# Layers 2 and 3 of a four-layer graph kernel take their chunks in the order 2, 3, 1, 0, so that layer 2 begins with the chunk that layer 1 ended on

## The chip, the cores and the metric

The kernel runs on one core of one Trainium2 chip. The metric is the device time of one execution in microseconds (us). A profiled execution has in addition a span, from its first to its last instruction, and a record of every instruction and DMA in it. Engines: PE multiplies matrices (PEld loads its weights), DVE is the vector engine, ACT the scalar engine, POOL is GpSimd, and SP issues most DMAs.

## The reference

Four layers work on the same 3327 nodes with 64 features. Each reads the same dense, weighted adjacency matrix `adj` (3327 x 3327, float32, 44 MB) in full, and each ends in a residual layer normalisation:

```python
x = layernorm(x + L0(x, adj, W))                 # mean over neighbours: (adj @ x) / (rowsum + 1)
x = layernorm(x + L1(x, adj, weight, bias))      # hyperbolic: sum over j of w[i,j] * logmap(x_i, x_j), expmap
x = layernorm(x + L2(x, adj, W, b))              # (adj @ x + x) / deg, concat, relu, unit norm
x = layernorm(x + L3(x, adj, weight, bias))      # the last 100 neighbours of each row, weights 0.5 ** rank

# L3
mask = (adj != 0); rank = cumsum(mask, axis=1)   # w = mask * 0.5 ** (k - pos) for the last 100 set places
out  = w @ (x @ weight) + bias
```

## The kernel before

**Tiles.** The matrix is transposed, padded to 3328 x 3328 and cut into four chunks of 832 columns (the nodes i whose sums are formed) by 26 blocks of 128 rows (the nodes j that are summed over). A *pair* is two row blocks of one chunk, [128, 2, 832] float32, 832 KB; one DMA on SP (`load_adj`, L278) fetches it into one of four `adj` buffers. A layer needs 4 x 13 pairs, and layers 0, 1 and 2 fetch all 52 each. `aggregate_pair` (L434) adds a pair to a chunk's sums in PSUM: four float32 products, eight records at L439, 1.40 us of PE.

**Layer 0** takes the chunks in `ORDER` (0, 3, 1, 2) and also makes the ranks of layer 3 for chunks 0, 1 and 2 (uint8, `rank`).

**Layer 1** (`layer1_far`, L785; the arm `layer1_near` isn't run on this input) goes over `ORDER` again, the pairs of each chunk in the order of `PAIRS` (0 to 5, 10, 11, 12, 6, 7, 8, 9). For each block PE makes v (L793) from `wt` and `ut`, DVE makes p (L804) from v and the pair, ACT and POOL or DVE make s (L817 to L819, L812), and PE adds s up (L824). p has 4 buffers, s has 9. At a chunk's end `keep1` (L832) copies the sums out, `own1` (L842, products at L847) makes a product with the nodes' own features from `ut`, and `epilogue1` (L853, products at L861) makes the new features of that chunk's nodes in `xr`. `GROUPS` says which blocks of nodes have both chunks they need: 0 to 5 with chunk 0, 20 to 25 with 3, 6 to 12 with 1, 13 to 19 with 2.

**Layer 2** needs all of `xr` to end a sum, but it can begin: nine of the 13 pairs of its first chunk (`EARLY`) don't touch the blocks of layer 1's last group, 13 to 19. `load_ahead2` (L1135) fetches the first six when layer 1 issues its last step, four into the `adj` buffers and two into `wt`; `begin2` (L1143) adds two of them (`BEGUN`) ahead of the last `epilogue1` and seven behind it. Then `layers_2_and_3` (L1153) goes over the chunks in `ORDER`, which starts with chunk 0. For each chunk it loads and adds pairs, `prologue2` (L1158) prepares the nodes' own part at the 11th pair, `keep_sums` copies the sums, and `epilogue2` (L1180, products at L1187) makes the input of layer 3, `x3`, and splits it into three bfloat16 `parts` (L1221 to L1224).

**Ranks of chunk 3** are made in layer 2, in its second chunk, over the pairs from 12 down to 0: `mask` (L459, DVE) marks the set places, `count` (L496, PE, L505) counts along the rows, `carry` (L491, DVE) hands a pair's count to the next, ACT writes the ranks (L515) into `uw`, which is `ut` and `wt`. `last_rows` (L521) mends the last row of each block by small DMAs on POOL (L530, L531, L537) and three DVE instructions (L533 to L535).

**Layer 3** consists of 52 *pieces* (`piece`, L1245): one pair of blocks of one chunk, twelve bfloat16 products (L1263) of `parts` with `bits`, which ACT or DVE expand from the ranks (L1242, L1243; ten buffers, tag `m16`, shared with the masks). A piece needs the `parts` of its two blocks for all columns. Twelve pieces lie between the pairs of layer 2's third chunk, eight in its fourth, and 32 behind it.

**Order.** The program is written as one sequence, with `issue_after` for wishes. At build a scheduler lays out the instructions of each engine, and buffer pools and PSUM banks (`Banks`) decide which must wait for which; each engine then works through its own list in order, and a waiting instruction holds what stands behind it. Memory of a pool that is closed is taken by the next pool, whose first users then wait for the last users of the old one.

Of the kernel before, what the change touches and what calls it, by code (L numbers as in the profile page):

```python
# [40 lines left out]
GROUPS = {0: (0, 6), 3: (20, 26), 1: (6, 13), 2: (13, 20)}  # L41
GB = 7
# [5 lines left out]
BEGUN = 2  # L48
# [56 lines left out]
LAST_PAIR = 9  # L105
# [3 lines left out]
def four_gnn_layers_kernel(  # L109
# [164 lines left out]
    def load_adj(c, jp, t=None):  # L274

        if t is None:
            t = adjp.tile([P, 2, CH], FP, name="adj", tag="adj")
# [35 lines left out]
    def blocks_of(c):  # L313
        return (*GROUPS[c], GROUPS[c][1] - GROUPS[c][0])

# [118 lines left out]
    def aggregate_pair(acc, x, a2, jp, first, last, behind=None):  # L434


        for k in (1, 0):
            for h in range(2):
                issued = nc.tensor.matmul(  # L439
                    acc[h * D : (h + 1) * D, 0:HC], lhsT=x[:, 2 * jp + k, 0:D],  # L440
                    rhs=a2[:, k, bass.ts(h, HC)],
# [6 lines left out]
    class Ranks:  # L448
# [8 lines left out]
        def mask(self, jp, a2):  # L457
            mask = self.mp.tile([P, 2, CH], U16, name="mask", tag="m16").bitcast(BF)
            issued = nc.vector.tensor_scalar(mask, a2, 0.0, None, op0=ALU.not_equal)  # L459
# [325 lines left out]
    def layer1_far(banks, begin2):  # L785

        with tc.tile_pool(name="l1w", bufs=1) as wp:

            def far_v(c, jb, after):
# [11 lines left out]
            def far_factors(v, a, engine):  # L801

                p = wp.tile([P, CH], FP, name="p", tag="p", bufs=4)
# [3 lines left out]
                s = wp.tile([P, CH], FP, name="s", tag="s", bufs=L1_AHEAD + 3)  # L807
# [85 lines left out]
            waiting, last, side, total, summed = [], None, None, NCH * NB, None  # L893
            for start in range(0, total + L1_AHEAD, L1_GROUP):
                group = range(start, start + L1_GROUP)
                made = []
                for i in group:
                    if i < total:
                        if i % 2 == 0:
                            c, jp, a2 = next(pairs)  # L900
                        jb = 2 * jp + i % 2
# [4 lines left out]
                for i in group:  # L906
# [12 lines left out]
                    if i == total - 1:  # L919
                        loaded2 = load_ahead2()  # L920
# [21 lines left out]
                for i in group:  # L942
# [6 lines left out]
                    if n == NCH - 1 and j >= NB - OWN1_LAST:  # L949
                        assert side is None  # L950
                        k = 3 * (j - NB + OWN1_LAST)
                        if k == 0:
                            own = banks.one(0)
# [3 lines left out]
            issued = summed  # L957
            issued = begin2(banks, 0, loaded2, issued)
            for done in epilogue1(ORDER[-1], own, 1, issued):
                pass  # L960
            begin2(banks, 1, loaded2, issued)
            return done
# [172 lines left out]
    def load_ahead2():  # L1135


        views = [None] * 4 + [
            wt[:, bass.ts(k, 2 * CH)].rearrange("p (b i) -> p b i", b=2) for k in range(2)
        ]  # L1140
        return [load_adj(ORDER[0], PAIRS[k], view) for k, view in enumerate(views)]

    def begin2(banks, part, loaded, behind, kept={}):  # L1143

        if part == 0:
            kept["acc"] = banks.pair(0)[:, 0, :]
        for i in range(0, BEGUN) if part == 0 else range(BEGUN, EARLY):
            jp = PAIRS[i]
            a2 = loaded.pop(0) if loaded else load_adj(ORDER[0], jp)
            issued = aggregate_pair(kept["acc"], xr, a2, jp, i == 0, False, behind)  # L1150
        return issued

    def layers_2_and_3(banks, acc, done):  # L1153

        with tc.tile_pool(name="late", bufs=1) as late, tc.tile_pool(name="l2m", bufs=10) as mp:
# [273 lines left out]
```

## Time and profile before

| what | value |
|---|---|
| median of 3 runs | 537.79 us (536.46 to 537.92) |
| profiled execution: time, span | 536.65 us, 534.9 us |
| read from HBM | 134.27 MB |
| loads of a pair | 156, of 832 KB |
| layer 1's last sum ends (L824), last epilogue's `xr` (L783) ends | 345.9 us, 365.9 us |
| layer 2's first chunk summed, first count of ranks starts | 374.5 us, 383.9 us |
| second chunk's products (L1187) start | 421.9 us |
| last pair added | about 482 us |

Times in the table's lower half are from the span's start. Groups of instructions are named by line, engine and operation, then output<-input. A row of the chain or timeline begins with the start and the duration in us. A busy PE is not a PE at its peak, since products overlap; the spacing of its records tells more. Where a wait has several causes, the profile names the last.

### The profile page before, as it was taken

The page shows a single profiled execution, that of the slowest core. Times are in us where ns is not written, and L with a number is a line of the kernel's source. Part 1 is how long each engine was busy: PE and PEld are TensorE (multiplying, and loading weights), DVE is VectorE, ACT ScalarE, POOL GpSimd, SP SyncE. Part 2 cuts the span into 40 slices and gives each one's busy share as a digit, 9 for nine tenths or more (in the row PEclk, how much of TensorE's full clock was granted, in tenths as well). Part 3 has the DMA queues.
Part 4 walks back from the last instruction along what each step waited for, and adds up shares of the span by engine and source line. Part 5 has one row for each costly group of instructions (what it writes and reads, how often), then busy time and mean ns, then how long its engine had stood idle before and what let it go on. Part 6 is the DMA issues. An engine that isn't in the chain of part 4 may idle for free.

```text
span 534.9 us, 8471 instructions
## 1 busy us (share of the span) xinstructions
PE 484.1 (90%) x3256; PEld 242.7 (45%) x3256; DVE 389.5 (73%) x707; ACT 334.1 (62%) x393; POOL 176.2 (33%) x150
## 2 busy tenths in 40 slices
PE   5999999998858999998999999997798999999993
PEld 3555444454423334433443353352344675656672
DVE  3575449899669888799789869945699972736834
ACT  1436536786868989788879977500278653236931
POOL 2001101112008888767767875221022020210000
PEclk9999999999989999999999999999999999999997
DMA  8899999899266777767767876879997789980012
GB/s 271 308 363 347 394 399 387 297 317 305 82 229 219 254 257 260 247 208 242 244 201 256 255 227 244 290 227 355 349 320 263 234 288 325 309 319 2 1 28 43
DMA packets 47172, 135.93 MB, mean 254 GB/s; under 512 B 6903, under 2 KB 7007, under 8 KB 47059
## 3 DMA queue, kind: packets, MB, share of 16 engines
q1 hardware_dynamic: 46594, 134.75, 73.6%
q0 software_dynamic: 384, 0.52, 0.4%
q8 instruction: 27, 0.44, 0.4%
q14 instruction: 23, 0.18, 0.1%
q10 hardware_dynamic: 144, 0.03, 0.0%
HBM read 134.27 MB, written 0.85 MB: 253 GB/s over the span
## 4 chain that ended last, share of the span: by engine, by line
PE 49%; DVE 27%; ACT 10%; DMA 6%; issue 3%; POOL 1%; ACTq 0%; POOLq 0%; DVEq 0%
PE one L439 14%; PE two L1263 10%; DVE p L804 7%; PE two L793 6%; DMA adj<-in_adjt_dram 6%; DVE mask L491 5%; PE one L824 5%; PE two L505 5%; DVE s L812 4%; DVE mask L459 3%; ACT s L817 3%; PE two L439 2%; ACT s L818 2%; ACT rank L515 2%; PE two L1187 1%
## 5 line engine op out<-in xcount | busy, mean ns | idle before, releaser
L819 POOL TENSOR_TENSOR s<-s,p 128x832 f32<-128x832 f32 x67 | 130.1, 1956 | 73.3 <-ACT s L818 61.4
L804 DVE SCALAR_TENSOR_TENSOR p<-two,adj 128x832 f32<-128x832 f32 x100 | 101.0, 1018 | 17.8 <-issue 13.3
L793 PE MATMUL two<-uw 64*128 64x416 f32 x416 | 90.1, 545 | 14.3 <-DVE s L812 7.2
L515 ACT ACTIVATE rank<-two,last_bias 128x832 uint8<-128x832 f32 x78 | 71.6, 952 | 45.5 <-DVE mask L491 22.8
L824 PE MATMUL one<-s,xu 128*64 128x416 f32 x416 | 85.2, 524 | 0.0
L439 PE MATMUL one<-adj,x0w 128*64 128x416 f32 x416 | 82.3, 523 | 2.3 <-ACT x0w L644 1.4
L817 ACT ACTIVATE s<-two,far_bias 128x832 f32<-128x832 f32 x67 | 63.7, 950 | 22.7 <-DVE p L804 20.7
L439 PE MATMUL one<-adj,xr 128*64 128x416 f32 x312 | 73.3, 515 | 3.1 <-DMA adj<-in_adjt_dram 3.1
L491 DVE SCALAR_TENSOR_TENSOR mask<-two,minus_last,mask 32x832 bf16<-32x832 f32 x48 | 52.5, 1093 | 24.4 <-PE two L505 20.0
L459 DVE TENSOR_SCALAR mask<-adj 128x1664 bf16<-128x1664 f32 x52 | 55.3, 1066 | 18.8 <-DMA adj<-in_adjt_dram 18.2
L793 PEld LDWEIGHTS two<-uw 64*128 64x128 f32 x416 | 37.5, 189 | 67.0 <-PE one L824 22.6
L1263 PE MATMUL two<-bits,parts 128*64 128x416 bf16 x624 | 67.7, 339 | 0.0
L505 PE MATMUL two<-mask,tri 128*64 128x416 bf16 x416 | 53.5, 346 | 10.9 <-DVE mask L491 8.3
L818 ACT ACTIVATE s<-s 128x832 f32<-128x832 f32 x67 | 60.1, 897 | 1.9
L1263 PEld LDWEIGHTS <-parts 128*64 128x64 bf16 x624 | 41.9, 110 | 20.4 <-issue 5.0
L824 PEld LDWEIGHTS one<-s,xu 128*64 128x64 f32 x416 | 25.8, 136 | 47.5 <-issue 46.6
L505 PEld LDWEIGHTS <-tri 128*64 128x64 bf16 x416 | 24.6, 110 | 45.9 <-issue 24.9
L439 PEld LDWEIGHTS one<-adj,x0w 128*64 128x64 f32 x416 | 29.4, 138 | 34.1 <-issue 23.5
L812 DVE SCALAR_TENSOR_TENSOR s<-two,p 128x832 f32<-128x832 f32 x37 | 37.6, 1016 | 3.0 <-ACT two L809 2.5
L439 PEld LDWEIGHTS one<-adj,xr 128*64 128x64 f32 x312 | 29.4, 137 | 22.4 <-issue 13.6
L1243 ACT ACTIVATE bits<-rank 128x1664 uint16<-128x1664 uint8 x21 | 32.3, 1579 | 9.9 <-PE two L1263 9.8
L809 ACT ACTIVATE two<-two,far_bias 128x832 f32<-128x832 f32 x37 | 34.0, 919 | 5.1 <-DVE p L804 4.9
(235 smaller groups left out, 453.0 us busy)
## 6 DMA issues: line engine op xcount, KB each, us to landing
adj<-in_adjt_dram SPq DMA_DIRECT2D x152, 832.0 KB, 5.6
sums<-in_adjt_dram SPq DMA_DIRECT2D x2, 832.0 KB, 6.0
uw<-in_adjt_dram SPq DMA_DIRECT2D x2, 832.0 KB, 6.5
uw<-in_xt_dram SPq DMA_DIRECT2D x1, 640.0 KB, 10.7
last_a<-in_adjt_dram POOLq DMA_DIRECT2D x4, 84.5 KB, 7.4
out_dram<-o SPq DMA_DIRECT2D x1, 224.0 KB, 3.7
uw<-in_xt_dram SPq DMA_DIRECT2D x1, 192.0 KB, 3.2
out_dram<-o SPq DMA_DIRECT2D x1, 192.0 KB, 2.3
```

The costliest lines, as they stand in the source:

```text
L439: issued = nc.tensor.matmul(acc[h * D : (h + 1) * D, 0:HC], lhsT=x[:, 2 * jp + k, 0:D], rhs=a2[:, k, bass.ts(h, HC)], start=(first and k = ...
L459: issued = nc.vector.tensor_scalar(mask, a2, 0.0, None, op0=ALU.not_equal)
L491: nc.vector.scalar_tensor_tensor(halves(last), ranks.after[P - 32 : P, :, 0:HC], minus_last[P - 32 : P, :], halves(last), op0=ALU.mult, op ...
L505: issued = nc.tensor.matmul(counts[k][rows, h, 0:HC], lhsT=lhsT[:, rows], rhs=mask[:, of, bass.ts(h, HC)], start=lhsT is tri, stop=(k == 1 ...
L515: nc.scalar.activation(halves(ranks.rank[:, 2 * jp + k, :]), counts[k][:, :, 0:HC], AF.Relu, bias=last_bias,)
L793: issued = nc.tensor.matmul(v[:, h, 0:HC], lhsT=wt[rows, bass.ts(jb, P)], rhs=ut[rows, bass.ds(c * CH + h * HC, HC)], start=True, stop=True,)
L804: issued = nc.vector.scalar_tensor_tensor(halves(p), v, 0.25 - 0.5 * FD, halves(a), op0=ALU.add, op1=ALU.mult)
L817: nc.scalar.activation(halves(s), v, AF.Square, bias=far_bias, scale=-2.0)
L818: nc.scalar.activation(s, s, AF.Copy, bias=FG)
L819: nc.gpsimd.tensor_mul(s, s, p)
L824: issued = nc.tensor.matmul(acc[h * D : (h + 1) * D, 0:HC], lhsT=xu[:, jb, 0:D], rhs=s[:, bass.ts(h, HC)], start=first, stop=last,)
L1263: issued = nc.tensor.matmul(acc3[c][h * D : (h + 1) * D, 0:HC], lhsT=parts[:, 2 * jp + b, bass.ts(part, D)], rhs=bits[:, b, bass.ts(h, HC) ...
```

## The change

`ORDER2` = (2, 3, 1, 0) replaces `ORDER` in layers 2 and 3, with groups of blocks to match. Layer 1 still ends with chunk 2; the pairs 6 to 9 of it, its last four, stay in the four `adj` buffers (`kept`) for layer 2's first chunk. Nine pairs are fetched ahead instead of six: three into `ut` and `wt` (the first as soon as its place is free), four as halves into buffers of p and s, two more into `ut`. Two pairs of the second chunk are fetched ahead as halves into buffers of the tag `m16`, whose pool now lies ahead of `late`. One pair instead of two is begun ahead of the last `epilogue1`, whose own product moves to another PSUM bank. The pieces of layer 3 change their order with the groups.

```diff
+ORDER2 = (2, 3, 1, 0)
+GROUPS2 = {2: (13, 19), 3: (19, 26), 1: (7, 13), 0: (0, 7)}
 GB = 7
...
-BEGUN = 2
+BEGUN = 1
...
 L3_BESIDE = 12
-LAST_PAIR = 9
+LAST_PAIR = 3
...
+        if isinstance(t, list):
+            for k in range(2):
+                nc.sync.dma_start(out=t[k], in_=adjt[c, 2 * jp + k])
+            return t
         if t is None:
...
-    def blocks_of(c):
-        return (*GROUPS[c], GROUPS[c][1] - GROUPS[c][0])
+    def blocks_of(c, groups=GROUPS):
+        return (*groups[c], groups[c][1] - groups[c][0])
...
         for k in (1, 0):
+            a = a2[k] if isinstance(a2, list) else a2[:, k, :]
             for h in range(2):
...
                     acc[h * D : (h + 1) * D, 0:HC], lhsT=x[:, 2 * jp + k, 0:D],
-                    rhs=a2[:, k, bass.ts(h, HC)],
+                    rhs=a[:, bass.ts(h, HC)],
                     start=(first and k == 1), stop=(last and k == 0),
...
             mask = self.mp.tile([P, 2, CH], U16, name="mask", tag="m16").bitcast(BF)
-            issued = nc.vector.tensor_scalar(mask, a2, 0.0, None, op0=ALU.not_equal)
+            if isinstance(a2, list):
+                for k, a in enumerate(a2):
+                    issued = nc.vector.tensor_scalar(
+                        mask[:, k, :], a, 0.0, None, op0=ALU.not_equal
+                    )
+            else:
+                issued = nc.vector.tensor_scalar(mask, a2, 0.0, None, op0=ALU.not_equal)
             self.masked.append([self, jp, mask, False])
...
+            def tile_p():
+                return wp.tile([P, CH], FP, name="p", tag="p", bufs=4)
+            def tile_s():
+                return wp.tile([P, CH], FP, name="s", tag="s", bufs=L1_AHEAD + 3)
...
-                p = wp.tile([P, CH], FP, name="p", tag="p", bufs=4)
+                p = tile_p()
                 issued = nc.vector.scalar_tensor_tensor(
...
                 )
-                s = wp.tile([P, CH], FP, name="s", tag="s", bufs=L1_AHEAD + 3)
+                s = tile_s()
                 if engine == "V":
...
             pairs = adj_pairs(first_pairs)
-            waiting, last, side, total, summed = [], None, None, NCH * NB, None
+            waiting, last, side, total, summed, kept = [], None, None, NCH * NB, None, {}
             for start in range(0, total + L1_AHEAD, L1_GROUP):
...
                             c, jp, a2 = next(pairs)
+                            if c == ORDER[-1] and jp in PAIRS[EARLY:]:
+                                kept[jp] = a2
                         jb = 2 * jp + i % 2
...
                     if i == total - 1:
-                        loaded2 = load_ahead2()
+                        loading = load_ahead2(lambda k: tile_p() if k < 4 else tile_s())
+                        loaded2 = next(loading)
                     if late is not None and i >= LATE_AT and not step(late, p_issued):
...
                         if k == 0:
-                            own = banks.one(0)
+                            own = banks.pair()[:, 0, :]
                         own1(ORDER[n], own, (k, k + 1, k + 2), summed)
...
                         keep1(ORDER[n], acc)
-            issued = summed
-            issued = begin2(banks, 0, loaded2, issued)
-            for done in epilogue1(ORDER[-1], own, 1, issued):
+            next(loading)
+            issued = begin2(banks, 0, loaded2, summed)
+            all_of(loading)
+            for done in epilogue1(ORDER[-1], own, banks.turns[1], issued):
                 pass
             begin2(banks, 1, loaded2, issued)
-            return done
+            return done, kept
...
-    def load_ahead2():
-        views = [None] * 4 + [
-            wt[:, bass.ts(k, 2 * CH)].rearrange("p (b i) -> p b i", b=2) for k in range(2)
-        ]
-        return [load_adj(ORDER[0], PAIRS[k], view) for k, view in enumerate(views)]
+    def load_ahead2(more):
...
+        def load(k, t):
+            return load_adj(ORDER2[0], PAIRS[k], t)
+        def view(t, k):
+            return t[:, bass.ts(k, 2 * CH)].rearrange("p (b i) -> p b i", b=2)
+        loaded = [load(k, view(*t)) for k, t in enumerate(((ut, 0), (wt, 0), (wt, 1)))]
+        yield loaded
+        places = [[more(2 * i + k) for k in range(2)] for i in range(4)]
+        loaded += [load(3 + k, t) for k, t in enumerate((*places, view(ut, 1)))]
+        yield
+        loaded.append(load(8, view(ut, 0)))
...
         if part == 0:
-            kept["acc"] = banks.pair(0)[:, 0, :]
+            kept["acc"] = banks.pair(banks.turns[0])[:, 0, :]
         for i in range(0, BEGUN) if part == 0 else range(BEGUN, EARLY):
-            jp = PAIRS[i]
-            a2 = loaded.pop(0) if loaded else load_adj(ORDER[0], jp)
-            issued = aggregate_pair(kept["acc"], xr, a2, jp, i == 0, False, behind)
+            issued = aggregate_pair(kept["acc"], xr, loaded[i], PAIRS[i], i == 0, False, behind)
         return issued
-    def layers_2_and_3(banks, acc, done):
-        with tc.tile_pool(name="late", bufs=1) as late, tc.tile_pool(name="l2m", bufs=10) as mp:
+    def layers_2_and_3(banks, acc, done, there):
+        with tc.tile_pool(name="l2m", bufs=10) as mp, tc.tile_pool(name="late", bufs=1) as late:
             parts = late.tile([P, NB, 3 * D], BF, name="parts")
...
-                b0, b1_, nb = blocks_of(c)
+                b0, b1_, nb = blocks_of(c, GROUPS2)
                 cols = bass.ds(b0 * P, nb * P)
...
                 issued = nc.vector.tensor_reduce(m[:, 0:nb], xs, axis=AX.X, op=ALU.add)
-                if c == ORDER[0]:
+                if c == ORDER2[0]:
                     issue_after(issued, done)
...
-                b0, b1_, nb = blocks_of(c)
-                work, alone = Work(nb), c == ORDER[-1]
+                b0, b1_, nb = blocks_of(c, GROUPS2)
+                work, alone = Work(nb), c == ORDER2[-1]
                 pb = per_block(banks.pair(2), nb, 2 * D)
...
                         for half in range(2):
-                            acc3[ORDER[which + 2 * half]] = two[:, half, :]
+                            acc3[ORDER2[which + 2 * half]] = two[:, half, :]
                     for ahead in range(BITS_AHEAD):
...
-            early = {2: (0, 1, 2), 3: (10, 11)}
-            pieces = [(c, jp) for jps in (*early.values(), (12, 3, 4, 5)) for jp in jps for c in ORDER]
+            early = {2: (7, 8, 9), 3: (10, 11)}
+            pieces = [(c, jp) for jps in (*early.values(), (12, 4, 5, 6)) for jp in jps for c in ORDER2]
             behind = 4 * len(early[2])
             pieces[0:behind] = sorted(pieces[0:behind], key=lambda piece: piece[0] == LATE_RANKS)
-            pieces += [(c, jp) for c in ORDER for jp in (6, 7, 8, LAST_PAIR)]
+            pieces += [(c, jp) for c in ORDER2 for jp in (0, 1, 2, LAST_PAIR)]
             left3 = len(pieces) - 4 * NCH
             beside = range(left3 - L3_LEFT + BITS_AHEAD, left3 - L3_LEFT + BITS_AHEAD + L3_BESIDE)
-            rows = last_rows(late, [(c, rank[:, c]) for c in ORDER if c != LATE_RANKS])
+            ahead = [
+                load_adj(
+                    ORDER2[1], jp, [mp.tile([P, CH], FP, name="a1", tag="m16") for _ in range(2)]
+                )
+                for jp in (NB // 2 - 1, NB // 2 - 2)
+            ]
+            rows = last_rows(late, [(c, rank[:, c]) for c in ORDER2 if c != LATE_RANKS])
             next(rows)
             k = 0
-            for n, c in enumerate(ORDER):
+            for n, c in enumerate(ORDER2):
                 if n > 0:
...
                         continue
-                    a2 = load_adj(c, jp)
+                    if n == 0 and jp in there:
+                        a2 = there.pop(jp)
+                    elif n == 1 and i < 2:
+                        a2 = ahead.pop(0)
+                    else:
+                        a2 = load_adj(c, jp)
                     issued = aggregate_pair(acc, xr, a2, jp, i == 0, i == NB // 2 - 1, counted)
...
                             all_of(rows)
-                    if n in early and i < 4 * len(early[n]):
+                    if n in early and 0 <= i - 3 + n < 4 * len(early[n]):
                         piece(k)
...
                     if n > 0 and i == (1 if n < NCH else 0):
-                        b0, b1_, nb = blocks_of(ORDER[n - 1])
+                        b0, b1_, nb = blocks_of(ORDER2[n - 1], GROUPS2)
                         halves3 = ((b0, b0 + 3), (b0 + 3, b1_)) if n == NCH else ((b0, b1_),)
...
                 if n < NCH:
-                    keep_sums(ORDER[n], acc3[ORDER[n]], 0, True)
+                    keep_sums(ORDER2[n], acc3[ORDER2[n]], 0, True)
...
             kept = {}
-            done = layer1_far(banks, lambda *args: begin2(*args, kept))
-            layers_2_and_3(banks, kept.pop("acc"), done)
+            done, there = layer1_far(banks, lambda *args: begin2(*args, kept))
+            layers_2_and_3(banks, kept.pop("acc"), done, there)
...
```

More of the change, by code (lines that the diff above doesn't have):

```diff
@@ L1381, in four_gnn_layers_kernel @@
             kept = {}
-            loaded = load_ahead2()
-            for part in range(2):
-                begin2(banks, part, loaded, None, kept)
-            layers_2_and_3(banks, kept.pop("acc"), done)
+            with tc.tile_pool(name="l2a_near", bufs=8) as more:
+                loading = load_ahead2(lambda k: more.tile([P, CH], FP, name="ahead", tag="ahead"))
+                loaded = next(loading)
+                next(loading)
+                begin2(banks, 0, loaded, None, kept)
+                all_of(loading)
+                begin2(banks, 1, loaded, None, kept)
+            layers_2_and_3(banks, kept.pop("acc"), done, {})
 def kernel(**inputs):
```

## The prediction

> **What bounds the kernel now.** I read the page first, for which engine is full.
>
> ```profile
> PE 484.1 (90%) x3256; PEld 242.7 (45%) x3256; DVE 389.5 (73%) x707; ACT 334.1 (62%) x393; POOL 176.2 (33%) x150
> PE 49%; DVE 27%; ACT 10%; DMA 6%; issue 3%; POOL 1%; ACTq 0%; POOLq 0%; DVEq 0%
> ```
>
> Over the whole span it is PE, but the 6% of DMA in the chain is a wait, and the change works on loads. So next the span in stages from the end of layer 1 (start:end, length, then busy time of PE, PEld, DVE, ACT, POOL, clock, DMA share, GB/s).
>
> ```profile
> 353.30:365.90 12.60, 10.15 (x56) 3.77 (x56) 9.86 (x36) 1.29 (x3) 3.92 (x7) 1.00 0.98 288
> 365.90:383.90 18.00, 13.53 (x76) 5.51 (x78) 8.97 (x15) 1.29 (x2) 2.19 (x4) 1.00 1.03 365
> 383.90:421.90 38.00, 34.04 (x262) 17.50 (x261) 36.59 (x53) 29.04 (x35) 5.52 (x6) 1.00 0.85 290
> 421.90:485.40 63.50, 63.42 (x493) 41.62 (x495) 34.17 (x64) 23.85 (x26) 10.05 (x10) 1.00 0.82 284
> ```
>
> From 353 to 384 the DMA engines are full and PE is not; from 384 to 422 DVE is full (36.6 of 38 us); from 422 on PE is full, at full clock. A microsecond won before 422 is therefore handed to the end unless a later stage gets a wait of its own. The chain in the first two stages (start, length, what):
>
> ```profile
> by line: DMA adj<-in_adjt_dram 52.4%; PE two L439 33.4%; PE one L439 5.2%; PE two L1187 5.0%; PE two L1165 2.5%; PE two L861 1.1%; PE two L505 0.9%; issue 0.4%
> ...
> 353.30 7.16 PE two L439 x40
> ...
> 360.48 8.05 DMA adj<-in_adjt_dram
> ...
> 368.57 1.62 PE two L439 x8
> ...
> 372.55 8.18 DMA adj<-in_adjt_dram
> ...
> 380.78 1.62 PE one L439 x8
> ```
>
> Loads that could only be issued when PE freed a buffer set the pace until 382, and layer 2's second chunk, which also counts ranks, starts on hungry buffers. Last, the two DVE groups that fill 385 to 421 (busy, mean ns | idle before):
>
> ```profile
> L491 DVE SCALAR_TENSOR_TENSOR mask<-two,minus_last,mask 32x832 bf16<-32x832 f32 x12 | 13.1, 1092 | 0.9 <-PE two L505 0.5
> L459 DVE TENSOR_SCALAR mask<-adj 128x1664 bf16<-128x1664 f32 x9 | 9.5, 1069 | 0.1
> ```
>
> **The change, part by part.** Times "after" are estimates: rows of this trace, moved along the instruction order that the two built programs have. All sums stand against the profiled execution (span 534.9, time 536.65); the median of the runs is 537.79, 1.1 higher, and I subtract from that.
>
> *Own products moved ahead, one pair begun instead of two.* Before: PE finishes layer 1's last L824 at 345.77, starts one pair (L439), waits for xr (L783) until 346.88 because the own product's bank is still held by the previous epilogue, does own1 (L847, 14 records, 1.7 us), finishes two pairs, and only then starts L861 at 351.52. After: own1 has a bank of its own; six of its seven products stand between the last L824s, which delays the last of these by 12 x 0.11 = 1.34 us, to 347.11. ACT's and DVE's copies (L427, L838: 346.86 to 347.95 before) move by as much, to 348.2 and 349.3. One pair (1.40) and the last own product fill PE meanwhile. L861 then starts at 348.8, 2.7 earlier, and its last four wait for 349.3. The DVE chain behind it (L868 at 353.34 to L783's end at 365.94: 12.6 us) is untouched, so xr of the last group is ready at 363.2.
>
> *Nine pairs fetched ahead, four kept.* Four loads of 832 KB go. The nine come into ut, wt and the spent p and s buffers. The first is queued in front of a layer-1 load; the own products and the POOL product it waits for end at 312.8 in this trace, and that layer-1 load is issued at 313.56, so I cost it nothing (if a load slips it has some 10 us: issued 313.56, used near 328). The others follow the last readers of their places: wt's second half at 340.3, the halves in p and s from 340.7 to 346.2 (after L812s), ut at 349.3 and 349.7. Queued loads of this trace land about 2.1 us apart, so they land at 344.7, 346.9, 349.0, 351.1, 353.2, 355.3 and 357.5; PE wants them at 351.8, 353.2 and every 1.4 us on. All are in time: PE's waits for loads, 2.5 us at 361 and 0.4 to 2 before each pair from 366 to 373, go. What is late next is xr: eight pairs end at 350.35 + 8 x 1.40 = 361.6, and PE idles 1.6 us until 363.2. The four kept pairs and the transposes (0.84) end at 369.7; before, the copy of the sums starts at 374.50. This is 4.8 us won.
>
> [...] The row: 832 KB take 4.4 us alone, 2.1 when queued, so loads overlap and the split costs SP's 0.37 us of issue. [...]
>
> *Two pairs of the second chunk ahead.* Their buffers lie where p and s lay; the four half loads wait on SP for the seventh pair (PE, 358.8), with all later loads behind them, and these need kept pairs freed after 364.6 anyway. The halves land at about 362.6 to 366; the next four pairs, issued as kept pairs are freed, at 369 to 375.
>
> *Rows on POOL and DVE.* POOL's memset (L528) ran at 355.2 after L874; now it waits for that same seventh pair, so the six small DMAs behind it start at 359.6 instead of 355.9 and the last is issued at 362.3. They took 7.3 to 7.6 us here beside a full queue, 4.7 for one at 389. So they land between 367.0 and 369.9; L534 and L535 stand on DVE ahead of the third mask and of the sums' copy, which the second-layer products (L1187) need, and these stand on PE ahead of the rest of the chunk. DVE needs about 8.5 us for all that from 363.2 by itself; with the wait the copy ends between 371.7 and 373.4. [...] The row at 389, amid masks on a full DVE, was issued in 0.51 us, as elsewhere: I take nothing.
>
> *Counting starts.* L1187 (1.6), then 3.15 us of pairs: counts start at 376.5 to 378.2 against 383.86. DVE's path to the first carry (L491) has 4.95 us after L1187: 378.3 to 380.0 against 385.15, so 5.2 to 6.9 won, 6.0 in the middle. And two masks and the front of the first epilogue, with an own row product (2.1 + 1.8 + 0.6, less one more "bits", 1.0: 3.5 us), are now done before the full DVE stretch, which was 35.6 us. Bounds for it: 32.0 if DVE stays full, 35.6 if PE, whose own work there is about 32 (13 counts of 1.05, 13 pairs of 1.40), turns the rest into waits. I take 33.6: 2.0 more. Sum 8.0.
>
> *Layer 3's first pieces.* The same 52 pieces (12 products, 1.05 us each) in another order. Half a pair more is done before they begin (-0.7), L1187 has seven blocks (+0.25). New: pair 9 has block 19, which belongs to the second chunk's group, so its pieces need that epilogue's parts (L1224), which were needed only a chunk later. Before, these were done 18.5 us after L1187 (423.4 to 441.9); PE now has 18.5 us of other work in front. Bounds 0 and 3, I take 0.45. Together 0. The tail is the same by count.
>
> **Rivals.** (a) *Hungry loads.* While the kept pairs fill all four buffers, no load of the second chunk but two can fly; its seventh pair's load is issued only at about 377.5. Landing after 4.6 us (the median from 384 to 422) it meets its mask at 382; after 8.0 (the median from 366 to 384) it is 3 us late, and the 2.0 of the stretch go as well: gain 3, 534.8. Against it: nothing else is queued then. (b) *More than I give.* PE has about 16 us of true idle from 346 to 422 (76.1 less 60 of work by the spacing of its records). If the DVE stretch takes 32.0, L1187 waits for nothing and pieces flow, 11 us: 526.8. (c) *Slower: block 19.* DVE has four and ACT two expansions of bits queued ahead of the parts, each waiting for a piece on PE, while PE waits for the parts. From 18.5 us on each microsecond is PE idle on the path; the 8.0 are lost at 26.5, and with 29 the time is 540.3. For it: the chain is new on the path and crosses three engines. Against: the last expansion in front waits for the sixth piece, 12.3 us after L1187, leaving 6 us for some 3 us of work. (d) *The order is not followed*: the built order shows 152 pairs' loads for 156; only waits could undo it.
>
> **How the numbers follow.** The gain of 8.0 gives 537.8 - 8.0 = 529.8. Chances: near the forecast (5.5 to 10.5) 0.55; more, (b), 0.13; less, (a), 0.19; within 0.3%, about what a measurement of this kernel can tell from no change (1.6 us), 0.06; slower, (c) or a layer-1 load slipping, 0.07. The range from 526.0 to 535.5 leaves out about 0.2.
>
> **What would show it.** Right: L783's last end near 363; no wait of L439 for DMA from 345 to 370 but for xr; the first L491 of layer 2 near 379, the last ending near 413; PE full behind it and the end 8 earlier. Wrong: L534 waiting for its rows past 370, masks waiting for loads around 382, or PE waiting for parts before pair 9's pieces.

## The result: about 6 us faster, and the profile after

The changed kernel takes 532.43 us (median of 8 runs, 530.35 to 535.17) beside 538.11 of the kernel before on the same chip: ratio 0.9886, 95% interval 0.985 to 0.9921. Of the 8.0 us forecast, 5.7 came. Its profiled execution has a span of 529.9 us (time 531.74), 5.0 less than before. Three of the kernels below had one execution each in a slower state; it is left out of their times.

The page's lines for the engines and the chain; then the stages (start:end, length, busy time of PE, PEld, DVE, ACT, POOL, clock, DMA share, GB/s), cut at the same work as the stages of before: the last epilogue's first DVE operation, xr ready, the first count of ranks, the second and the third chunk's products.

```profile
PE 482.1 (91%) x3256; PEld 237.7 (45%) x3256; DVE 386.2 (73%) x709; ACT 334.6 (63%) x393; POOL 177.3 (33%) x150
...
PE 46%; DVE 25%; ACT 10%; DMA 8%; issue 6%; POOL 2%; DVEq 0%; POOLq 0%; ACTq 0%
```

```profile
351.30:363.90 12.60, 11.25 (x64) 4.36 (x62) 9.90 (x36) 1.29 (x3) 3.92 (x7) 1.00 0.71 257
363.90:380.60 16.70, 13.81 (x73) 7.09 (x75) 11.35 (x21) 2.38 (x4) 3.14 (x4) 0.90 0.83 277
380.60:417.65 37.05, 34.78 (x269) 18.50 (x266) 32.88 (x48) 29.86 (x35) 5.39 (x6) 1.00 0.85 284
417.65:481.30 63.65, 62.64 (x488) 35.85 (x490) 33.42 (x64) 22.30 (x25) 10.37 (x10) 1.00 0.81 280
```

The page hardly moves; the stages tell. In the first, PE is now busy for 11.25 of 12.6 us (before, 10.15), and what is missing is the wait for xr at its end: the early pairs no longer wait for loads. In the second it is not full (13.81 of 16.7), and its granted clock is 0.90. DVE isn't full in the third (32.88 of 37.05). Two waits are left on PE ahead of the counts (a timeline: start, length, operation, in brackets the idle time before it and what ended it):

```profile
363.92 3.01 PE L448 MATMUL two<-adj,xr 128*64 128x416 f32 x16 [1.37 <-DVE xr L798]
...
374.92 2.90 PE L1220 MATMUL two<-wl,sums 128*128 128x128 f32 x12 [2.87 <-DVE sums L435]
```

The first is the wait for xr that was forecast. The second was not, at this length: L1220 (L1187 before) waits for DVE to copy the sums. Before, DVE had waited for PE at this copy, and the products took 1.60 us:

```profile
374.50 0.58 DVE L427 COPY sums<-two 64x416 f32<-64x416 f32 x1 [4.21 <-PE two L439]
...
382.33 1.60 PE L1187 MATMUL two<-wl,sums 128*128 128x128 f32 x12
```

DVE's timeline after, up to that copy:

```profile
367.40 0.59 DVE L470 TENSOR_SCALAR mask<-a 128x832 bf16<-128x832 f32 x1 [1.99 <-DMA a<-in_adjt_dram]
...
370.24 0.59 DVE L548 TENSOR_SCALAR last_a<-last_a 78x832 f32<-78x832 f32 x1 [1.20 <-DMA last_a<-in_adjt_dram]
...
373.14 1.02 DVE L474 TENSOR_SCALAR mask<-adj 128x1664 bf16<-128x1664 f32 x1
374.19 0.58 DVE L435 COPY sums<-two 64x416 f32<-64x416 f32 x1
```

PE had the sums ready at 370.5. DVE came to the copy at 374.19, because its list has three things in front that need transfers: the third half of a mask (a wait of 1.99 us), the rows (L548 to L550, before L533 to L535; a wait of 1.20), and the mask of the third pair, whose load had landed at 372.22. The chain of waits runs through just this place:

```profile
359.88 0.79 POOL last_more L543
...
362.79 7.33 DMA last_a<-in_adjt_dram
370.24 0.60 DVE last_a L548
...
374.19 0.59 DVE sums L435
374.78 0.14 issue
374.92 2.92 PE two L1220 x12
```

And L1220 then takes 2.90 us for twelve records. The windows ahead of it and over it give the reason: PE is empty in the first (0.13 us busy of 3), and in the second the clock is about halved (0.54).

```profile
372.00:375.00 3.00, 0.13 (x2) 0.11 (x1) 2.94 (x6) 0.19 (x1) 1.49 (x3) 0.89 1.03 403
375.00:378.00 3.00, 3.00 (x14) 2.72 (x16) 0.97 (x2) 0.31 (x1) 0.93 (x1) 0.54 0.81 292
```

Last the two DVE groups of the stretch from the first carry to the last, as shown of before: the waits for loads have not gone (1.8 us of masks), but the twelve carries fit into 34.0 us (382.55 to 416.52) instead of 35.6.

```profile
L506 DVE SCALAR_TENSOR_TENSOR mask<-two,minus_last,mask 32x832 bf16<-32x832 f32 x12 | 13.1, 1093 | 1.5 <-PE two L520 1.2
L474 DVE TENSOR_SCALAR mask<-adj 128x1664 bf16<-128x1664 f32 x8 | 8.2, 1024 | 1.8 <-DMA adj<-in_adjt_dram 1.8
```

### The profile page after: what moved, and what is told of

It reads as the page before. It is cut to its first block, busy times and chain, and to the rows that moved or that the text cites. A ratio compares the mean times of both kernels' runs of the same rounds, so it can differ in the third digit from the quotient of the medians.

```text
span 529.9 us, 8500 instructions
## 1 busy us (share of the span) xinstructions
PE 482.1 (91%) x3256; PEld 237.7 (45%) x3256; DVE 386.2 (73%) x709; ACT 334.6 (63%) x393; POOL 177.3 (33%) x150
## 4 chain that ended last, share of the span: by engine, by line
PE 46%; DVE 25%; ACT 10%; DMA 8%; issue 6%; POOL 2%; DVEq 0%; POOLq 0%; ACTq 0%
PE one L448 12%; PE two L1296 10%; DVE p L825 7%; DMA adj<-in_adjt_dram 6%; PE two L814 6%; PE one L845 6%; DVE mask L506 4%; ACT s L838 3%; PE two L520 3%; DVE s L833 3%; DVE mask L474 3%; ACT s L839 2%; PE two L448 2%; ACT rank L530 2%; PE two L1220 2%
## 5 line engine op out<-in xcount | busy, mean ns | idle before, releaser
L814 PE MATMUL two<-uw 64*128 64x416 f32 x416 | 88.5, 537 | 14.8 <-DVE s L833 7.2
L448 PE MATMUL one<-adj,x0w 128*64 128x416 f32 x416 | 82.7, 524 | 2.6 <-ACT x0w L659 1.4
L448 PE MATMUL one<-adj,xr 128*64 128x416 f32 x296 | 65.6, 514 | 0.9 <-DMA adj<-in_adjt_dram 0.9
L474 DVE TENSOR_SCALAR mask<-adj 128x1664 bf16<-128x1664 f32 x50 | 51.9, 1038 | 18.1 <-DMA adj<-in_adjt_dram 17.4
L1296 PE MATMUL two<-bits,parts 128*64 128x416 bf16 x624 | 64.2, 340 | 0.0
L1296 PEld LDWEIGHTS <-parts 128*64 128x64 bf16 x624 | 37.4, 110 | 23.6 <-issue 6.6
L448 PEld LDWEIGHTS one<-adj,x0w 128*64 128x64 f32 x416 | 29.1, 138 | 35.1 <-issue 23.4
L448 PEld LDWEIGHTS one<-adj,xr 128*64 128x64 f32 x296 | 26.0, 137 | 19.1 <-issue 13.8
```

The costliest lines, as they stand in the source:

```text
L448: issued = nc.tensor.matmul(acc[h * D : (h + 1) * D, 0:HC], lhsT=x[:, 2 * jp + k, 0:D], rhs=a[:, bass.ts(h, HC)], start=(first and k == 1) ...
L814: issued = nc.tensor.matmul(v[:, h, 0:HC], lhsT=wt[rows, bass.ts(jb, P)], rhs=ut[rows, bass.ds(c * CH + h * HC, HC)], start=True, stop=True,)
L1296: issued = nc.tensor.matmul(acc3[c][h * D : (h + 1) * D, 0:HC], lhsT=parts[:, 2 * jp + b, bass.ts(part, D)], rhs=bits[:, b, bass.ts(h, HC) ...
```

## The experiments

**How they are compared.** Layer 1 starts up to 6.5 us earlier or later in one profile than in another, for reasons ahead of the change. So the places in the traces below are counted from the start of layer 1's first sum (165.5 us into the span before, 165.3 after). Time and ratio are of the timed runs, each beside the kernel before on the same chip. The other columns are from one profile of each kernel, and two profiles of one kernel (after and after_again, copy_first and copy_first_2) differ by up to 1.3 us. Line numbers shift by a few between kernels.

| kernel | xr ready | products (L1187, L1220) start | first carry | last carry ends | last instruction | time, us | ratio to before (95%) |
|---|---|---|---|---|---|---|---|
| before | 200.4 | 216.8 | 219.6 | 255.2 | 369.4 | 538.1 | |
| before_with_own | 198.6 | 214.0 | 218.6 | 253.7 | 368.2 | 537.6 | 0.9972 (0.995, 0.9995) |
| after | 198.6 | 209.7 | 217.3 | 251.3 | 364.7 | 532.4 | 0.9886 (0.985, 0.9921) |
| after_again | 198.5 | 209.5 | 217.4 | 250.9 | 363.5 | 533.3 | 0.9891 (0.9855, 0.9927) |
| own_as_before | 204.8 | 215.8 | 221.7 | 256.5 | 368.4 | 534.6 | 0.9901 (0.9858, 0.9943) |
| own_as_before_2 | 200.4 | 210.9 | 216.0 | 252.0 | 363.6 | 532.0 | 0.9857 (0.9813, 0.9902) |
| no_pairs_ahead | 198.6 | 206.8 | 217.7 | 250.9 | 365.5 | 534.1 | 0.9909 (0.9874, 0.9944) |
| not_kept | 198.5 | 209.7 | 216.1 | 249.7 | 364.0 | 532.3 | 0.9891 (0.9852, 0.9931) |
| rows_in_xu | 198.5 | 207.3 | 215.6 | 249.3 | 361.3 | 530.3 | 0.9862 (0.9821, 0.9904) |
| rows_in_xu_copy_first | 198.6 | 206.8 | 216.4 | 250.0 | 363.2 | 530.5 | 0.985 (0.9819, 0.988) |
| rows_early_back_late | 199.9 | 208.1 | 215.0 | 247.5 | 365.1 | 532.8 | 0.9891 (0.9854, 0.9928) |
| copy_first | 198.5 | 206.6 | 213.9 | 247.2 | 359.9 | 529.4 | 0.9821 (0.9785, 0.9856) |
| copy_first_2 | 199.4 | 207.5 | 214.7 | 247.6 | 361.3 | 529.9 | 0.982 (0.977, 0.9871) |
| copy_first_not_kept | 198.6 | 206.6 | 215.8 | 250.0 | 365.0 | 533.7 | 0.9894 (0.9856, 0.9932) |

My theory: what is missing of the forecast is lost between xr and the first carry, by DVE's list ahead of the sums' copy, above all by the rows. Rivals: the second chunk's loads hold the stage in any case; the clock.

**Rows gathered early.** The rows' tiles move into `xu`, which nobody reads after layer 1's last sum.

```diff
-        a = pool.tile(shape, FP, name="last_a")
-        more = pool.tile(shape, U8, name="last_more")
+        if pool is None:
+            flat = xu.rearrange("p b f -> p (b f)")
+            a = flat[0 : shape[0], 0:CH]
+            more = flat[0 : shape[0], CH : CH + CH // 4].bitcast(U8)
+        else:
...
-            rows = last_rows(late, [(c, rank[:, c]) for c in ORDER2 if c != LATE_RANKS])
+            rows = last_rows(None, [(c, rank[:, c]) for c in ORDER2 if c != LATE_RANKS])
```

> The changed kernel, but the last rows of the three ranked chunks are gathered in xu, which nobody needs from 347 on, instead of behind the mask buffers, so their memset and six small DMAs start at about 350 instead of 359.6. Theory rows (they set the start of L1220, 2.9 us late, and take queue time from the second chunk's first loads): the wait of VectorE for last_a goes, the third half of a mask waits under 1 us instead of 2.0, the sums' copy ends near 371.7 instead of 374.8, L1220 starts near 372, takes 1.6 us again instead of 2.9, the first carry comes near 378.5 to 380 instead of 382.55, and the end is 2.5 to 4 us earlier: 528.5 to 530. Rival loads (the third pair's load, landed at 372.2 and masked ahead of the copy, is what holds it): the copy ends at 373.5 or later and under 1.2 us are won. Rival clock (L1220's 2.9 us has nothing to do with the wait in front): it stays at 2.9.

The wait for last_a went, the wait for the third half of a mask fell to 1.01 us, the copy ended 8.7 us after xr instead of 10.9, L1225 waited 0.6 us on PE instead of 2.9 and took 1.58. But the first carry came only 1.6 us earlier, because in front of it DVE now waited 1.91 us for the load of the second chunk's sixth pair, and the time, 530.3, stayed just above the 528.5 to 530 expected. The theory holds for the copy; behind it the rival is next.

**The copy first.** On DVE, the third pair's mask is put behind the sums' copy, the rows' three operations behind that mask:

```diff
                         mask = ranks.mask(jp, a2)
+                        if i == 2:
+                            issue_after(mask, copied)
+                            step(rows, mask)
+                            all_of(rows)
...
-                        if n == 0:
-                            step(rows, made)
-                            all_of(rows)
...
-                keep_sums(c, acc, D, True)
+                copied = keep_sums(c, acc, D, True)
```

> The changed kernel, but on VectorE the sums' copy stands ahead of the third pair's mask and of the rows' three operations, which follow later amid the masks; the rows' DMAs stay where they are. Theory rows (it is the order on VectorE by which late rows reach TensorE): the copy ends near 371.1, L1220 starts without a wait near 372 and takes 1.6 us; the 2.2 us of the rows' operations then fall on the full VectorE, so the first carry comes near 380.5 instead of 382.55, and 1 to 2.5 us are won: 530 to 531.5. If the rows or loads hold the stage by themselves and not through the copy, the first carry stays at 382 to 383 and nothing is won (within 0.7 us).

> The kernel with the copy ahead of mask and rows on VectorE once more, on another chip: again 3 us or more below the changed kernel (ratio to before 0.980 to 0.985), no wait of over 2 us on TensorE but none of its clock falls between 363 and 420, L1223 in 1.6 us.

PE's timeline of copy_first: no wait in front of L1223, and 1.60 us for it.

```profile
367.30 3.01 PE L451 MATMUL two<-adj,xr 128*64 128x416 f32 x16 [1.37 <-DVE xr L801]
...
373.86 1.56 PE L451 MATMUL one<-a,xr 128*64 128x416 f32 x6
375.35 1.60 PE L1223 MATMUL two<-wl,sums 128*128 128x128 f32 x12
```

DVE's timeline of the same kernel, up to the first carry:

```profile
374.08 0.58 DVE L436 COPY sums<-two 64x416 f32<-64x416 f32 x1 [0.48 <-PE two L451]
374.78 1.03 DVE L477 TENSOR_SCALAR mask<-adj 128x1664 bf16<-128x1664 f32 x1
375.72 0.58 DVE L551 TENSOR_SCALAR last_a<-last_a 78x832 f32<-78x832 f32 x1
...
378.36 1.01 DVE L552 SCALAR_TENSOR_TENSOR last_a<-last_more,last_a 78x832 f32<-78x832 uint8 x1
...
382.57 1.09 DVE L509 SCALAR_TENSOR_TENSOR mask<-two,minus_last,mask 32x832 bf16<-32x832 f32 x1
```

Now the copy waits for PE, not PE for the copy. The first carry comes 15.3 us after xr in both runs (18.7 and 18.9 in the changed kernel), 1.3 better than the expected move of 2.0 although the same rows are mended in front of it. At 529.4 and 529.9 us, on two chips, these are the lowest medians of the study: about 3 us below the changed kernel, at the edge of what the intervals separate. From rows_in_xu the intervals don't separate it.

**Both.** Rows in `xu` where the program had them, and the third mask behind the copy.

> Both: the rows gathered early in xu, and the sums' copy ahead of the third pair's mask on VectorE. Theory rows: L1220 starts within 0.3 us of TensorE's being free, near 372, the first carry at 378 to 379, the last carry's end near 412 to 413, which is what the prediction gave, and the time is 528 to 529.5, up to 1 us better than the rows moved alone. Rival loads: with the front gone the masks wait for the loads issued after 377, the stretch from first to last carry grows from 34.0 to 36 or more, and under 2 us are won.

L1228 started 8.2 us after xr with a wait of 0.05 us, as expected; yet the first carry came 17.9 us after xr, and PE's wait was only moved:

```profile
385.25 0.54 PE L523 MATMUL two<-mask,tri 128*64 128x416 bf16 x4 [2.80 <-DVE mask L509]
```

DVE in turn waited 1.97 us for the sixth pair's load. That load took 9.0 us from issue to landing in the changed kernel, 9.2 with the rows early, 10.0 here, but 7.0 in copy_first, where the rows' way back into `rank` (L552) is issued at 380 and later instead of at 374. So the rival is right for this kernel, and there is a guess at why the load is late.

**Rows early, way back late.**

```diff
-        for k, (c, r) in enumerate(chunks):
+        yield None
+        yield [
             nc.gpsimd.dma_start(out=r[P - 1 : P, :, :], in_=more[k * NB : (k + 1) * NB, :])
+            for k, (c, r) in enumerate(chunks)
+        ]
...
+                        if i == 8:
+                            step(rows, mask)
+                            all_of(rows)
```

(`more` lies in `y_last` here, since `xu` is written again before the late transfer.)

> As with the rows gathered early and the copy in front, but the rows' way back into rank (three small DMAs, each into one partition) goes out behind the first epilogue of layer 2, at about 390, instead of at 374. There the load of the second chunk's sixth pair took 9.2 to 10 us from issue to landing with them beside it, and 7.0 in the kernel where they came later. Theory contention: that load lands in 7.5 us or less, VectorE no longer waits 2 us for it ahead of the first carry, which comes 15 to 16 us after xr's end instead of 17.9, and the time is 1.5 to 2.5 us below that kernel's, 528 to 529. Rival (the loads are late by themselves, because they are issued late): the load still takes 9 us or more, first carry at 17.5 or later, time 530 to 531.

The load took 6.9 us and the first carry came 15.05 us after xr: that agrees with the guess of contention. The time does not follow: 532.8. Three things differ from copy_first. xr is ready 1.4 us later; `more`'s memset and three DMAs now stand among POOL's products in layer 1, but copy_first_2, without them, has xr 0.9 later too, so that isn't shown to be their price. DVE, with the last carry at 247.5, is 5.0 us ahead of the next products (252.5; 2.2 in copy_first), for which it then waits: behind the counts PE is the bound. And in the third chunk PE waits twice for loads that took 8.0 and 8.1 us to land, which it does not in copy_first:

```profile
439.11 1.62 PE L451 MATMUL one<-adj,xr 128*64 128x416 f32 x8 [1.66 <-DMA adj<-in_adjt_dram]
441.22 1.26 PE L451 MATMUL one<-adj,xr 128*64 128x416 f32 x5 [0.50 <-DMA adj<-in_adjt_dram]
```

These 2.2 us, with the 2.8 more at the products, are about the 4.9 us by which this profile is longer than copy_first's from the last carry to the end. Why these loads were slow is open.

**Not kept.** The four pairs loaded again, behind the nine.

```diff
...
+            there = {jp: load_adj(ORDER2[0], jp, after=sent[-1]) for jp in there}
             ahead = [
```

> The changed kernel, but the four pairs of layer 1's last chunk are loaded again, behind the nine fetched ahead and in front of the second chunk's two pairs. If the change's gain comes from keeping (the four loads removed hold up what is queued behind them): they land at about 361, 363, 365 and 368, still in time for TensorE, but the second chunk's first masks land some 8 us later, at 372 to 376, VectorE's copy of the sums stands behind them, and 2 to 4 us of the 5 to 6 won are lost (534 to 536.5). If the gain comes from the nine pairs ahead and the earlier own products alone, DMA has room and the time stays within 0.7 us of the changed kernel's 532.4.

No loss: 532.3 us. But DVE's list is another. With the loads later, the scheduler put the copy ahead of the masks of the second chunk:

```profile
373.09 0.58 DVE L441 COPY sums<-two 64x416 f32<-64x416 f32 x1
373.71 2.73 DVE L476 TENSOR_SCALAR mask<-a 128x832 bf16<-128x832 f32 x4
```

PE, too, did most of the second chunk's first two pairs (14 records of 16) ahead of the products, so that no long wait and no fall of the clock (1.00 from 340 to 526) stood there. Two edits in one, then; so keeping was tried again with the copy ahead of the third pair's mask in both kernels.

> The copy first, and the four pairs of layer 1's last chunk loaded again. In the run without keeping, VectorE's order differed (the copy stood ahead of the masks there), so that run gave up the four kept pairs and got the better order for it, and the two could have cancelled. If so, with the copy first in both, keeping shows its worth: the second chunk's first pairs land some 6 to 8 us later, the first carry comes 1.5 to 3 us later against xr than in the kernel with the copy first (15.3), and the time is 1 to 3 us above it. If keeping is worth nothing, both come within 0.7 us.

The second chunk's third to sixth pairs took 10.1 to 11.0 us to land, the first carry came 17.1 us after xr instead of 15.3, and the time was 533.7, 3.8 us above copy_first_2 on the same chip, again at the edge of the intervals. Keeping is worth something, then, once the copy comes first. The lists are not quite equal here either (without keeping, the copy stands ahead of all four mask halves), and what keeping is worth with the copy behind the masks, as in the changed kernel, no run shows.

**The own products as before.** The bank is `banks.one(0)` again and `BEGUN = 2`.

> The changed kernel, but layer 1's last own products wait again for the bank of the previous epilogue, behind the first of two pairs begun. Theory xr: from the last L845 to the end of xr (L798) it takes 2.1 us longer than in the changed kernel, everything behind moves with it, and the time rises by 1.5 to 2.3 us, to 534 to 534.7. Rival: rows and loads hold the front of the second chunk anyway, first carry does not move against the last L845, and under 0.7 us are lost.

Inconclusive: three masks moved ahead of xr's last operation, the third waited 2.7 us, and xr was ready 6.2 us later, not 2. With the masks held behind xr:

> The changed kernel without that first part, as in the run of this kind before, but with the second chunk's first masks kept behind xr's last operation on VectorE: there two of them had moved in front of it and waited 2.7 us for their loads, and the clock fell besides. Now xr comes 2 us later against the start of layer 1 than in the changed kernel. Theory xr: everything behind moves with it and 1.3 to 2.3 us are lost (534 to 535). Rival (rows and loads, which do not start from xr, set the pace): the first carry moves by under 0.7 us, time 532 to 533.

xr 1.8 us later, and nothing lost: 532.0, as the rival has it. But this is no clean removal. PE's wait for the copy was 1.83 us there, and L1221 took 1.57 at full clock instead of 2.90; and a mask (1.02 us) that stands ahead of the first carry in the changed kernel stands behind it here. With both, the first carry came 1.3 us earlier, and the last 0.7 later. The other way round, this part alone on the kernel before:

```diff
-BEGUN = 2
+BEGUN = 1
...
-                            own = banks.one(0)
+                            own = banks.pair()[:, 0, :]
```

> The kernel before with the first part of the change alone: a bank of its own for layer 1's last own products, and one pair begun instead of two; order, loads and all else as before. xr should be ready 2 us earlier against the start of layer 1. Theory loads (before, the pairs' loads set the pace from 363 to 382, so an earlier xr only lengthens the waits for them): the first carry moves by under 0.7 us and the time stays within 0.3%. Rival (xr sets the pace, and this part pays by itself): 1.5 to 2.1 us faster, ratio 0.996 to 0.997.

xr 1.8 us earlier, first carry 1.1, the time 1.2 below (ratio 0.9972): between the two. The pairs' loads swallowed less than half of it.

**No pairs of the second chunk ahead.**

```diff
-                for jp in (NB // 2 - 1, NB // 2 - 2)
+                for jp in ()
```

> The changed kernel without the second chunk's two pairs in mask buffers: all its loads go to the four buffers that the kept pairs hold. Theory loads: the first two land at about 370 and 372, the fifth is issued only when the first has been used, the masks ahead of the first carry are complete some 4 us later, and the time rises by 2.5 to 4.5 us, to 535 to 537, most of the gain gone. Rival (rows and the copy hold the stage, loads do not): L1220 stays where it is against xr's end (11.0 us behind it), and under 1 us is lost.

No loss is shown: 534.1, 0.7 us above after_again on the same chip and well within the intervals. Neither side came as described. The products started 2.9 us earlier, since no masks stood in front of the copy, and the rows' DMAs, with nothing beside them, took 2.2 to 2.5 us instead of 6.1 to 7.7. Then PE waited 2.53 us for a load and the clock fell again (0.50); the first carry was only 0.4 us later.

**The changed kernel again.**

> The changed kernel once more, unedited. Theory clock as a stray: each profile so far has one stretch with a granted clock of 0.90 to 0.97, in 150 to 200 us everywhere but in the changed kernel's profile, where it fell on 363 to 380; if that is chance, L1220's twelve records take 1.6 us here, the dip is back before 200, and the time stays at 532.4 within 0.7. Theory clock as a result of TensorE's idle time ahead of L1220: 2.9 us again, at the same place.

The clock dipped near the start of layer 1, as in most of the other profiles (0.83 from 140 to 160), and it fell at L1220 as well (0.53), which took 2.65 us. So in both profiles it came behind the wait:

```profile
378.00:381.00 3.00, 3.00 (x14) 2.56 (x16) 1.23 (x2) 0.30 (x1) 0.92 (x1) 0.53 0.77 267
```

## Why the prediction was right, and where it was too high

*Own products ahead.* Expected xr 2.7 us earlier; it was 1.8 from the start of layer 1 (2.1 in the span). The six products between the last sums delay these by 1.9 us, not 1.34: a step of six took 0.81 to 0.85. How much of it reaches the end is open: before_with_own passed on 1.1 of its 1.8 us, own_as_before_2 lost nothing, with another list and no fall of the clock.

*Nine ahead, four kept.* Right. The pairs landed from 344.5 to 359.1, all in time; PE waited for xr only, 1.37 us for 1.6 forecast; the halves landed 1.05 us apart, 2.1 a pair, the pace of queued whole pairs before, so no cost of the split shows in it. The kept pairs ended at 370.5 for 369.7. That keeping, and not only fetching, was needed is shown only by the pair copy_first and copy_first_not_kept. The nine pairs fetched early and the order itself, the core of the change, were not taken away in any run: that they make the gain rests on the waits that are gone from the trace (seven waits of PE for a load, of 0.3 to 1.7 us each, between 361 and 381 before; none there after).

*Rows on POOL and DVE.* This is the step that was off in size. The rows landed at 366.7 to 370.3, as forecast (367.0 to 369.9), and issuing them wasn't held up (0.51 us each, 0.69 the first, as before). But I let the copy end between 371.7 and 373.4, from one wait; there were two in a row (1.99 us for the half of a mask, 1.20 for the rows), and the copy ended at 374.77. The waiting for rows past 370, one of the signs of being wrong, came by a little: until 370.24. *Counting starts* took this over: the first carry was to come at 378.3 to 380.0, middle 379.15, and came at 382.55, 3.4 late. About in sum: 0.7 is xr, 1.5 the copy beyond that (2.2 from the middle of its range), and 1.3 the length of L1220, 2.9 for 1.6. That term was missing.

It could have been asked for: the trace of before has a stretch of 3.41 us at half clock, from 153.64, and in the 3.41 us ahead of it PE was busy for only 1.05, between waits. The length of one wait doesn't settle it. Gaps of 2.87 us (the changed kernel), 2.76 (after_again), 2.53 (no_pairs_ahead) and 2.23 (own_as_before) were each followed by a clock of 0.50 to 0.54; gaps of 1.88 and 1.83 in own_as_before_2 and of 1.74 before, at 363.57, were not; and 2.80 us ahead of the counts in rows_in_xu_copy_first was not either (1.00 from 382.5 to 388). So of the wait that my range left to PE (0.6 to 2.3 us, with a pair of 1.40 done behind the kept ones) only the upper end comes to a gap that a fall followed, while a copy 1.4 us past that range (374.77 for 373.4) cost 2.7.

Where a wait falls counts too, as the traces of before and after show. Each has one stretch at half clock ahead of its last 20 us; it lasts 3.41 us, and the one at the end of the trace begins 110 times (before) and 44 times (after) 3.41 us behind it. Counted in windows of 3.41 us from the start of that stretch, PE was idle for 2.37 us (before) and 2.29 us (after) of the window ahead of it, and for 1.80 us at most of any other from 60 to 512 us, behind which the clock stayed full. In the changed kernel:

```profile
370.92:374.33 3.41, 1.13 (x6) 0.19 (x2) 3.38 (x6) 0.00 (x0) 0.82 (x2) 1.00 1.03 403
374.33:377.74 3.41, 2.82 (x12) 2.64 (x12) 1.47 (x2) 0.50 (x1) 1.60 (x2) 0.50 0.89 332
```

The same three waits, of 1.51, 0.89 and 1.71 us near 150, stand in both traces. Before, one window (150.23 to 153.64) holds the 0.89 and most of the 1.71, and the clock halved; after, the windows there have at most 1.71 us of idle PE, and it did not. Whether the 2.80 us of rows_in_xu_copy_first passed for the same reason was not shown.

*The stretch of carries.* 34.0 us for 33.6 forecast (32.0 to 35.6), 33.5 in the second profile. In all kernels with the new order but rows_early_back_late (32.5) and own_as_before_2 (35.9, with a mask more in it) it was 32.9 to 34.9, wherever it began, and 35.1 to 35.6 with the old: the win here doesn't hang on the front.

*Layer 3's first pieces.* Forecast 0; from the last carry's end (4.2 us won) to the end of the span (5.0), 0.8 were won. This cannot be told from no change: from the last carry to the end the kernels with the new order took 111.6 to 117.6 us, the changed one 113.4 and, in its second profile, 112.6, beside 114.2 before. No wait for block 19's parts shows: PE is busy 62.64 of 63.65 us there. Rival (c) didn't come.

*Rival (a), hungry loads,* was half there: a load was issued at 370.70 and the next only at 381.49, and masks waited 1.8 us in all. It is next in line behind the rows, as rows_in_xu and both show.

So: 8.0 = 6.0 + 2.0 was forecast, and in the profile 2.6 + 1.6 + 0.8 = 5.0 came (5.7 by the medians), 0.2 of the 2.6 ahead of layer 1's sums. That the medians reach the case I held likeliest, 5.5 to 10.5, is in part luck: it is by 0.2 us, and after_again, on another chip, gained 5.1.

## What to carry to other kernels

When loads come early, look at what an in-order engine has in its list ahead of the one short copy that others wait for: a scheduler puts the early data's work in front, and it may wait for transfers there. Sum all waits in that list, not the last one. Where PE is idle for over 2 us of some 3.4 (2.29 and 2.37 here), allow for a slow restart: it cost 1.1 to 1.4 us (2.65 and 2.90 for the 1.60 of L1220, 3.04 for the 1.62 of a pair in no_pairs_ahead). Before crediting a part of a change, take it away with the order of the lists held fixed: here DVE's list changed in all five removals from the changed kernel, and what a part is worth in that kernel stayed open.

## What the runs showed of the hardware

The rows' small DMAs issued from POOL landed after 2.2 to 2.5 us with no load beside them (no_pairs_ahead) and after 6.1 to 7.7 behind queued loads (the changed kernel). Three of 21 KB, each into one partition, coincided with 2 to 3 us more for an 832 KB load beside them (9.0 to 10.0 us, against 6.9 and 7.0 where they were issued later); they are not the only cause of slow loads, since in copy_first_not_kept, where they also came later, four loads behind a fuller queue took 10.1 to 11.0. The clock fell to half (0.50 to 0.54) behind waits of PE of 2.23, 2.53, 2.76 and 2.87 us in four traces, and not behind one of 2.80 in a fifth. In before and after the one such stretch ahead of the last 20 us lasted 3.41 us, with 2.37 and 2.29 us of idle PE in the 3.41 us in front. Records of PE overlap: one of L439 or L448 lasts 0.51 us, and the eight of a pair, back to back, 1.62 from the first start to the last end.
